# The start of a causal attention and feed-forward kernel: the first eight heads' q and k laid out by selection products, and the rest of the preparation put beside the first steps

## The chip, the core and the metric

The kernel runs on one core of a Trainium2 chip. The metric is device microseconds of one execution. A core has five engines, each with a queue of its own that it works through in order: PE (TensorE, the matrix products; its weight loads are listed as PEld), DVE (VectorE), ACT (ScalarE), POOL (GpSimd) and SP (SyncE, which here only issues transfers). PE writes to PSUM, eight banks of 512 float32 for each of 128 partitions; DVE and ACT read it there.

## The reference

x has 4096 tokens of 256 features. The attention has 16 heads of 16 features:

```python
x = x + layernorm(attention(layernorm(x)))      # causal, softmax(q k^T / 4) v, then w_proj, b_proj
h = silu((y @ w1.T) * w1_s) * ((y @ w2.T) * w2_s)     # y = layernorm(x)
h = gelu((h @ h1.T) * h1_s); h = gelu((h @ h2.T) * h2_s)
x = x + layernorm((h @ w3.T) * w3_s)
```

The feed-forward weights are ternary, w_attn and w_proj are float32, and the biases of the attention are random.

## The kernel before

**Blocks and items.** The tokens are cut into eight blocks j of 512 (NB = 8). The attention goes through 32 items (j, g): block j of the queries with the four heads of group g. An item has `count` = 4 (j + 1) steps, one for each tile of 128 keys. A step makes the scores of its four heads (two ScoreUnits of two heads, L641 to L693: products of k and q, then a product that subtracts the row's maximum, then ACT's exponential) and, two steps later, their products with v (Values, L695 to L727). The feed-forward (L910 on) follows after all items.

**Maxima.** The row maxima come from products of their own, by MaxUnit (L569 to L639): two products of 64 rows into two of the three banks of the pool ps_m, and DVE's maximum over each (L594, or L598 with the mask on the diagonal). Two units, one for each pair of heads, make a pair of the stream `maxima`. Pairs run ahead of the scores: `goal` (L874) lets the stream reach three pairs (LEAD) past the end of the next item, spread evenly over the item's steps. When an item's last pair is done, `to_rows` (L625) turns its maxima into a row with four products (pmt) and a copy (mrow, L638).

**The preparation of a block** is the generator `prep(j)` (L498 to L555): load x, take the layernorm statistics (DVE for blocks 0 and 1, ACT for the others), normalize (DVE for block 0, POOL for the rest), transpose on PE into xT (tile T), and then `features` (L421) for k and q, each in two halves c of eight heads, and the products pv with wv for v. `features` makes 128 features for 512 tokens, adds the bias on ACT (tile full), and splits the result into hi and lo, two parts that the fast product format holds exactly. Each part is written twice to a DRAM array `halves_of` by SP (L449), four transfers of 256 KB for each half c: a score product wants for each head the rows hi, lo, hi, lo of k against hi, hi, lo, lo of q, 64 rows a head. `load_rows` (L453) reads two heads, 128 rows, back into one tile: `queries` two tiles for an item, `keys` two tiles for an item and a key block, into a ring of 16 slots (tags k0_0 to k15_1). `queries` of item n + 2 is called at the head of item n, and `ask` (L484) loads keys up to item n + 2. All these loads and sends stand in SP's one queue.

**Order.** Past L786 the order of each engine's queue is the order of the program text (a schedule written out by hand). Before the change it is: the product of v's bias with wp, added to bp (L829 to L838); prep(0); queries and keys for items 0 and 1; prep(1), all of it; seven pairs of maxima (L847); then the items (L852). Within an item, `Background` (L23) holds generators (preparations, projections) with a size in pieces; `bg.pace` (L898) advances as many pieces after each step as are needed to be done in time. A generator can yield BESIDE between products, where `unit_beside` (L816) may put a unit of maxima (only for blocks 1 to 6). prep(j + 2) is added in block j's first item at its third step and has to be done at the head of block j's last item (L855). project(j) (L208), the output projection, is added when the block's last values are stored.

Records: a float32 product appears in the profile as two records, so 16 records named pk and pq are eight products, the k and q features of one block.

Of the kernel before, what the change touches and what calls it, by code (L numbers as in the profile page):

```python
# [10 lines left out]
F32 = mybir.dt.float32  # L11
# [56 lines left out]
def sandwich_kernel(  # L68
# [116 lines left out]
    def piece(tag, name, dtype=F32):  # L185
        return pieces.tile([P, QB], dtype, tag=tag, name=name)
# [151 lines left out]
    with ExitStack() as actx:  # L338
# [13 lines left out]
        def two_banks(name):  # L352
            return ps_s.tile([P, 2, QB], F32, tag="s", name=name)

        class Room:
# [5 lines left out]
            def features(self, j):  # L361
                return [wk1.tile([P, DC, QB], F32, tag=t, name=f"{t}o_{j}") for t in ("o", "T")]
# [4 lines left out]
        wqk = [piece(f"wqk{d}", f"wqk{d}") for d in range(DC)]  # L367
        for d in range(DC):
            nc.scalar.dma_start(out=wqk[d], in_=w_attn[d * P : (d + 1) * P, 0 : 2 * D])
        wv = aw.tile([P, DC, D], F32, tag="wv", name="wv")  # L370
        nc.scalar.dma_start(
            out=wv, in_=w_attn[:, 2 * D : 3 * D].rearrange("(c p) f -> p c f", p=P)
        )

        bv = aw.tile([P, DC], F32, tag="bv", name="bv")
        nc.scalar.dma_start(out=bv, in_=b_attn[2 * D : 3 * D].rearrange("(c p) -> p c", p=P))

        bqk = aw.tile([P, 2 * DC], F32, tag="bqk", name="bqk")
        nc.scalar.dma_start(out=bqk, in_=b_attn[0 : 2 * D].rearrange("(s p) -> p s", p=P))
        nc.vector.tensor_scalar(bqk[:, 0:DC], bqk[:, 0:DC], SCALE, None, ALU.mult)  # L380

        two = aw.tile([P, 2], F32, tag="two", name="two")
        nc.vector.tensor_reduce(
            two,
            ident.rearrange("p (i pr e) -> p pr i e", i=2, pr=2)[:, :, :, 0:2],
            AX.XY,
            ALU.add,
        )
        identr = aw.tile([P, P], F32R, tag="identr", name="identr")
        nc.vector.tensor_copy(identr, ident)  # L390
        ones = [aw.tile([P, P], F32R, tag=f"ones{pr}", name=f"ones{pr}") for pr in range(2)]
        for pr in range(2):
            nc.vector.tensor_copy(ones[pr], two[:, pr : pr + 1].to_broadcast([P, P]))

        nc.scalar.dma_start(out=wp, in_=w_proj.rearrange("(c p) f -> p c f", p=P))
        nc.scalar.dma_start(out=bp, in_=b_proj.partition_broadcast(P))

        mask = aw.tile([P, QB], F32, tag="mask", name="mask")
        nc.gpsimd.memset(mask, 0.0)
# [18 lines left out]
            for j in range(NB)  # L418
        }

        def features(j, s, c, engine):  # L421

            i = "qk".index(s)
            ps = two_banks(f"p{s}_{j}_{c}")[:, 0, :]
            for d in range(DC):
                nc.tensor.matmul(  # L426
                    ps,
                    lhsT=wqk[d][:, i * D + c * P : i * D + (c + 1) * P],
                    rhs=xTs[j][:, d, :],
                    start=(d == 0),  # L430
                    stop=(d == DC - 1),
                )
                yield Background.BESIDE
            full = piece(f"full{c % 2}", f"full{s}_{j}_{c}")
            nc.scalar.activation(
                full,
                ps,
                AF.Identity,
                bias=bqk[:, i * DC + c : i * DC + c + 1],
                scale=1.0 if i else SCALE,  # L440
            )
            hi = piece(f"hi{c % 2}", f"hi{s}_{j}_{c}")
            engine.tensor_copy(hi.bitcast(F32R), full)
            lo = piece(f"lo{c % 2}", f"lo{s}_{j}_{c}")
            engine.tensor_tensor(lo.bitcast(F32R), full, hi.bitcast(F32R), ALU.subtract)
            for half, part in enumerate((hi, lo)):
                for d in range(2):
                    at = (d, half) if i else (half, d)
                    nc.sync.dma_start(  # L449
                        out=halves_of[s, j][8 * c : 8 * (c + 1), at[0], at[1]], in_=part  # L450
                    )

        def load_rows(tag, name, key, j, h):  # L453

# [7 lines left out]
        def query(tag, name, dtype):  # L462
            return qp.tile([P, QB], dtype, tag=tag, name=name)
# [31 lines left out]

        xTs = {}

        def prep(j, engine=nc.gpsimd):  # L498

            xj = xb[j] if j in xb else load_block(j)  # L500
            for _ in range(3):
                yield True
            mv = stat.tile([P, NT, 2], F32, tag="mv", name=f"mv_{j}")
            ahead = j < 2
            for t in range(NT):
                if ahead:
                    layernorm_stats(xj[:, t, :], mv, t)
                else:
                    mean_of(xj[:, t, :], mv, t)
                    yield True  # L510
                    spread_of(xj[:, t, :], mv, t)
                yield True
            v_j = kv.tile([P, NT, H * VW + HD], F32, tag=f"v{j}", name=f"v{j}")
            vb.append(v_j)
            nc.gpsimd.memset(v_j[:, :, H * VW :], 0.0)
            v_heads = v_j[:, :, 0 : H * VW].rearrange("p t (h e) -> p t h e", e=VW)
            nc.gpsimd.memset(v_heads[:, :, :, HD:VW], 1.0)
            rstd = (layernorm_rstd if ahead else rstd_of)(mv)
            for t in range(NT):
                (normalize if ahead else shift_and_scale)(  # L520
                    xj[:, t, :], xj[:, t, :], mv, rstd, t, engine
                )
                yield True
            for _ in range(3):
                yield True
            xT = xTs[j] = wk1.tile([P, DC, QB], F32, tag="T", name=f"xT_{j}")
            ps = two_banks(f"pt_{j}")
            for c in range(DC):
                for t in range(NT):
                    nc.tensor.transpose(  # L530
                        ps[:, c, t * P : (t + 1) * P], xj[:, t, c * P : (c + 1) * P], ident
                    )
            nc.scalar.copy(xT, ps)  # L533
            yield True
            for s in "kq":
                for c in range(DC):
                    yield from features(j, s, c, engine)
                    yield True
            for half in range(0, NT, 2):
                ps = two_banks(f"pv_{j}_{half}")[:, 0, :].rearrange("p (t f) -> p t f", t=2)  # L540
                for t in range(2):
                    for c in range(DC):
                        nc.tensor.matmul(  # L543
                            ps[:, t, :],
                            lhsT=xT[:, c, (half + t) * P : (half + t + 1) * P],
                            rhs=wv[:, c, :],
                            start=(c == 0),
                            stop=(c == DC - 1),
                        )
                    yield Background.BESIDE  # L550
                nc.scalar.copy(
                    v_heads[:, half : half + 2, :, 0:HD],
                    ps.rearrange("p t (h d) -> p t h d", d=HD),
                )
                yield True  # L555
# [260 lines left out]
        def unit_beside():  # L816
# [4 lines left out]
            if begun_pair:  # L821
                issue(MaxUnit(*begun_pair.pop(0)))

        values = Values()
        W = {}
        alone = cycle((False, False, True))
        issued = now = 0

        ps = two_banks("pb")[:, 0, 0:D]  # L829
        for c in range(DC):  # L830
            nc.tensor.matmul(
                ps,
                lhsT=bv[:, c : c + 1].to_broadcast([P, P]),
                rhs=wp[:, c, :],
                start=(c == 0),
                stop=(c == DC - 1),
            )
        nc.vector.tensor_tensor(bp, bp, ps, ALU.add)  # L838
        for j in range(2):
            work = prep(j, (nc.vector, nc.gpsimd)[j])  # L840
            while bg.piece(work) is not False:
                pass
            if j == 0:
                for n in range(2):
                    queries(*items[n])
                    keys(*chunks[n])
        while issued < first[1] + LEAD:  # L847
            for args in next(stream):
                issue(MaxUnit(*args))
            issued += 1  # L850
        rows_of(now + 4)
        for n, (j, g) in enumerate(items):  # L852
            if n + 2 < len(items):
                queries(*items[n + 2])
            if g == G - 1 and j + 2 < NB:  # L855
                bg.finish(("prep", j + 2))

            if (j, g) == (NB - 2, 0):
# [15 lines left out]
            goal = min(first[min(n + 2, len(items))] + LEAD, first[-1])  # L874
            for kt in range(count[n]):
                ask(n, kt)
                if (g, kt) == (0, 2) and j + 2 < NB:
                    bg.add(("prep", j + 2), prep(j + 2), PREP)
                due = begun + (goal - begun) * (kt + 1) // count[n] - issued
                pairs = [next(stream) for _ in range(due)]  # L880
# [14 lines left out]
                now += 2  # L895
                values.add(j, g, kt, max(kt - NT * j, 0) * P, es, now - 1)
                rows_of(now)
                bg.pace(count[n] - kt + count[n] * max(G - 2 - g, 0))  # L898
                if j > 0 and kt % 4 == 2 and kt < NT * j:
                    next(halving, None)  # L900
            rows_of(now + 2)
# [232 lines left out]
```

## Time and profile before

| | us |
|---|---|
| three runs | 2493.22, 2483.43, 2488.50 |
| median | 2488.5 |
| the profiled execution: its time | 2495.86 |
| its span, first to last instruction | 2494.2 |
| PE busy (share of the span) | 2395.7 (96%) |
| DVE busy | 1786.7 (72%) |
| ACT busy | 1309.1 (52%) |
| POOL busy | 561.6 (23%) |
| mean granted clock of PE | 0.975 |

The profile is of one execution. A line of its timeline has the start in us, the length in us, the engine (SPq and ACTq are the transfers that these engines issue), the line of the kernel, the operation, out<-in, and how many were merged; in brackets stands how long the engine was idle before it and what ended that wait. In the windows, each engine's busy time in a stretch is followed by the number of its instructions; the clock is what PE was granted, 1.00 being full. A busy PE may run at half rate. The page's slices cut the span into 40 equal parts of 62.4 us, with the busy share and the clock in tenths.

### The profile page before, as it was taken

Reading aid. Unit: us, or ns where it says so; the run is one execution under the profiler, and the core shown is the slowest. Engines: PE = TensorE matmul, PEld = TensorE weight load, DVE = VectorE, ACT = ScalarE, POOL = GpSimd, SP = SyncE. Lnnn points to the kernel's source line nnn. Section 1 sums busy time; section 2 is a strip of 40 time slices with the busy share of each in tenths; the row PEclk is TensorE's granted clock in tenths of the full one; section 3 lists DMA queues with packets and bytes.
Section 4 is the critical chain, followed back from the end, with each engine's and each line's share of the span. In section 5 each row is a group of like instructions: output and inputs, shape, how many; then the busy total and the mean of one; then the engine's idle time right before and its main releaser. Section 6 shows DMA issues by size and latency. Waiting matters only on the chain.

```text
span 2494.2 us, 40139 instructions
## 1 busy us (share of the span) xinstructions
PE 2395.7 (96%) x15237; PEld 1434.2 (58%) x15237; DVE 1786.7 (72%) x3838; ACT 1309.1 (52%) x1710; POOL 561.6 (23%) x898
## 2 busy tenths in 40 slices
PE   4899999999999999999999999999999999999998
PEld 2545545545554555455555555544488787887887
DVE  1667988888897989799999888986145535554553
ACT  1336666665675667666667667766822222222221
POOL 2325333423343233322422222000001200000000
PEclk8779999999999999999999999999999999999999
DMA  4444434323333322424222231111111100000000
GB/s 145 150 141 141 151 115 152 120 82 130 107 126 117 116 72 96 151 94 133 84 74 72 88 109 60 51 56 56 47 54 35 34 1 18 17 17 1 17 9 10
DMA packets 134825, 202.73 MB, mean 81 GB/s; under 512 B 14912, under 2 KB 59584, under 8 KB 134624
## 3 DMA queue, kind: packets, MB, share of 16 engines
q1 hardware_dynamic: 132672, 198.75, 24.3%
q8 instruction: 122, 2.00, 0.3%
q10 hardware_dynamic: 1776, 1.18, 0.2%
q14 instruction: 79, 0.65, 0.1%
q0 software_dynamic: 176, 0.15, 0.1%
HBM read 137.91 MB, written 62.13 MB: 80 GB/s over the span
## 4 chain that ended last, share of the span: by engine, by line
PE 82%; DVE 11%; issue 2%; DMA 2%; ACT 1%; POOL 1%; SPq 0%; ACTq 0%; POOLq 0%; DVEq 0%
PE av L714 20%; PE s L664 18%; PE z L1007 18%; PE pm L581 16%; DVE mx L594 3%; DVE pm L598 2%; PE pyf L1076 2%; DVE fa L1048 2%; PE pk L426 1%; PE py L249 1%; PE pv L543 1%; PE pq L426 1%; PE pmt L630 1%; PE za L1007 1%; PE zb L1007 1%
## 5 line engine op out<-in xcount | busy, mean ns | idle before, releaser
L679 ACT ACTIVATE e<-s 128x1024 f32<-128x1024 f32 (+3 forms) x1175 | 1039.1, 936 | 471.1 <-PE s L664 462.3
L594 DVE TENSOR_REDUCE mx<-pm 128x1 f32<-128x512 f32 x1792 | 1111.5, 682 | 153.0 <-PE pm L581 135.4
L581 PE MATMUL pm<-k,q 64*128 64x512 f32 (+3 forms) x2304 | 626.9, 456 | 33.0 <-DVE mx L594 18.6
L581 PEld LDWEIGHTS pm<-k,q 64*128 64x128 f32 x2304 | 325.1, 188 | 533.3 <-DVE mx L594 368.9
L714 PE MATMUL av<-e,v 128*32 128x512 f32 (+3 forms) x4608 | 582.5, 577 | 0.2 <-POOL e L684 0.2
L664 PE MATMUL s<-q,k 64*128 64x512 f32 (+3 forms) x2304 | 472.7, 391 | 4.4 <-ACT xT L533 1.2
L664 PE MATMUL s<-mrow,ones 64*128 64x512 f32 (+3 forms) x2304 | 458.9, 381 | 0.0
L598 DVE CUSTOM_DVE_ANT_0 pm<-pm,mask 128x384 f32<-128x384 f32 (+3 forms) x512 | 240.2, 517 | 78.6 <-PE pm L581 75.7
L1063 ACT ACTIVATE fb<-z,sh 128x512 f32<-128x512 f32 x128 | 88.1, 688 | 388.4 <-PE z L1007 367.2
L664 PEld LDWEIGHTS s<-q,k 64*128 64x128 f32 x2304 | 236.5, 189 | 71.7 <-issue 18.8
L664 PEld LDWEIGHTS s<-mrow,ones 64*128 64x128 f32 x2304 | 241.3, 189 | 38.3 <-DVE mrow L638 0.7
L684 POOL TENSOR_SCALAR_AFFINE_SELECT e<-e 128x256 f32<-128x256 f32 x256 | 102.3, 407 | 620.1 <-ACT e L679 618.0
L1007 PE MATMUL z<-hb_0h,h 128*128 128x512 f32 x512 | 200.8, 392 | 0.0
L1007 PE MATMUL z<-hb_0l,h 128*128 128x512 f32 x512 | 200.0, 391 | 0.0
L714 PEld LDWEIGHTS av<-e,v 128*32 128x32 f32 x4608 | 91.7, 108 | 143.6 <-issue 130.5
L173 POOL TENSOR_TENSOR rstd<-ve,neghalf 128x4 f32<-128x4 f32 (+1 forms) x22 | 20.7, 943 | 662.9 <-DVE ve L171 637.4
L977 DVE CAST hb_1h<-fb 128x512 fp32r<-128x512 f32 x64 | 27.8, 435 | 144.5 <-ACT fb L1063 144.5
L977 DVE CAST hb_0h<-fb 128x512 fp32r<-128x512 f32 x64 | 27.3, 427 | 138.7 <-ACT fb L1063 138.7
L1007 PEld LDWEIGHTS z<-hb_0h,h 128*128 128x128 f32 x512 | 96.8, 189 | 20.0
L1046 ACT ACTIVATE sl<-za,s 128x512 f32<-128x512 f32 x64 | 44.0, 689 | 122.2 <-PE za L1007 64.2
L1007 PEld LDWEIGHTS z<-hb_0l,h 128*128 128x128 f32 x512 | 96.7, 189 | 19.9
L1048 DVE SCALAR_TENSOR_TENSOR fa<-zb,s,sl 128x512 f32<-128x512 f32 x64 | 47.6, 745 | 72.2 <-ACT sl L1046 72.2
(247 smaller groups left out, 2437.8 us busy)
## 6 DMA issues: line engine op xcount, KB each, us to landing
k<-k SPq DMA_DIRECT2D x288, 256.0 KB
q<-q SPq DMA_DIRECT2D x64, 256.0 KB
x<-in_x_dram SPq DMA_DIRECT2D x16, 512.0 KB
k<-hik SPq DMA_DIRECT2D x32, 256.0 KB
k<-lok SPq DMA_DIRECT2D x32, 256.0 KB
q<-hiq SPq DMA_DIRECT2D x32, 256.0 KB
q<-loq SPq DMA_DIRECT2D x32, 256.0 KB
avd<-av_sb SPq DMA_DIRECT2D x32, 256.0 KB
```

Source lines behind the costliest of these rows:

```text
L426: nc.tensor.matmul(ps, lhsT=wqk[d][:, i * D + c * P : i * D + (c + 1) * P], rhs=xTs[j][:, d, :], start=(d == 0), stop=(d == DC - 1),)
L581: nc.tensor.matmul(ps[:, 0:n], lhsT=qT[j, g][pr][r, t * P : (t + 1) * P], rhs=kT[G * j + g, c, pr][r, 0:n], start=True, stop=True,)
L594: nc.vector.tensor_reduce(self.mx[:, h, c : c + 1], ps[:, 0:n], AX.X, ALU.max)
L598: nc.vector.tensor_tensor_reduce(out=ps[:, 0:n], in0=ps[:, 0:n], in1=mask[:, QB - n : QB], scale=1.0, scalar=-3.0e38, op0=ALU.add, op1=ALU ...
L664: nc.tensor.matmul(self.ps[i][:, self.q0 :], lhsT=(self.k, ones[pr])[m][r, :], rhs=(qT[j, g][pr], mT[j, g])[m][r, self.q0 :], start=(m == ...
L679: nc.scalar.activation(e[:, at : at + n, q0:], ps[:, :, q0:], AF.Exp)
L684: nc.gpsimd.affine_select(out=at, in_=at, compare_op=ALU.is_ge, fill=0.0, base=0, pattern=[[0, 2], [1, P]], channel_multiplier=-1,)
L714: nc.tensor.matmul(self.av[h * HW : (h + 1) * HW, q0:], lhsT=vb[kt // NT][:, kt % NT, o : o + HW], rhs=es[h // 2][:, h % 2, q0:], start=(k ...
L977: nc.vector.tensor_copy(hi, full)
L1007: nc.tensor.matmul(ps, lhsT=w[c], rhs=single(part[:, c, :]), start=(c == 0 and i == 0), stop=(c == kc - 1 and i == parts - 1),)
L1048: nc.vector.scalar_tensor_tensor(h, zb, s2[:, oc : oc + 1], sl, ALU.mult, ALU.mult)
L1063: nc.scalar.activation(h, z, AF.Gelu, scale=sc[:, oc : oc + 1])
```

## The change

1. The product that adds v's bias to bp goes from the head of the program into a function `bias_of_v`, called at item 1. Its inputs wp, bv and bp are no longer loaded on ACT's queue at the start but on SP's, after q of block 0. The q and k biases (bqk) are loaded before wv. The small constants (`two`, `identr`, `ones`, and the scaled bqk, now on ACT) are made after block 0's transposes.
2. `prep` is cut into `turned` (load to transposes), the features, and `values_of`. Only block 0 takes its statistics on DVE now.
3. Block 0's k and q of heads 0 to 7 (c = 0) don't go through DRAM to items 0 and 1. `at_home` multiplies hi and lo by `sel`, matrices of zeros and ones, in products of 32 rows (two heads of 16 features) and adds hi's and lo's product in PSUM, so that each of four banks gets the 128 rows of a pair of heads in their final order. ACT and DVE copy the banks to the tiles of items 0 and 1. k of these heads is still sent to DRAM, for the later blocks, q isn't. sel, hi and lo borrow slots 13 to 15 of the ring of keys.
4. `rest` makes c = 1 of k and q (POOL splits them) and v of block 0, with two units of maxima at each BESIDE, for the first five pairs of the stream (before: seven pairs, with nothing beside).
5. prep(1) becomes background work of items 0 and 1. prep(2) is added at item 2 instead of item 0 and has to be done at the head of item 6 instead of item 3. The pace is counted by `ends`.

The diff, cut to its core:

```diff
-        nc.scalar.dma_start(out=wp, in_=w_proj.rearrange("(c p) f -> p c f", p=P))
-        nc.scalar.dma_start(out=bp, in_=b_proj.partition_broadcast(P))
...
-        def features(j, s, c, engine):
+        def features(j, s, c, engine, tags=None, then=send):
...
+            then(j, s, c, (hi, lo))
...
-            ahead = j < 2
+            ahead = j < 1
...
+        def ends(n):
+
+            if n < G:
+                return first[2] if n < 2 else first[G + 2]
+            return first[max(n, n // G * G + G - 2) + 1]
...
+        sel = piece("k13_0", "sel", F32R)
+        nc.gpsimd.memset(sel.bitcast(F32), 0.0)
+
+        def select():
+            row = piece("k13_1", "row")[:, 0:HW]
+            nc.vector.tensor_reduce(row, ident.rearrange("p (m c) -> p c m", m=4), AX.X, ALU.add)
+            rows2 = row.rearrange("p (i d) -> p i d", i=2)
+            for i in range(2):
+                for half in range(2):
+                    at = (2 * i + half) * P
+                    to = sel[:, at : at + P].rearrange("p (i a b d) -> p i a b d", i=2, a=2, b=2)
+                    for e in range(2):
+                        a, b = (e, half) if i else (half, e)
+                        nc.vector.tensor_copy(to[:, :, a, b, :], rows2)
+
+        def at_home(j, s, c, parts):
+
+            i = "qk".index(s)
+            banks = [two_banks(f"home{s}_{n}") for n in range(2)]
+            for half, part in enumerate(parts):
+                at = (2 * i + half) * P
+                for m in range(4):
+                    r = slice(32 * m, 32 * (m + 1))
+                    nc.tensor.matmul(
+                        banks[m // 2][:, m % 2, :],
+                        lhsT=sel[r, at : at + P],
+                        rhs=part.bitcast(F32R)[r, :],
+                        start=(half == 0),
+                        stop=(half == 1),
+                    )
+            for n in range(2):
+                for pr in range(2):
+                    if i:
+                        t = kT[n, 0, pr] = piece(f"k{n}_{pr}", f"k{n}_0_{pr}", F32R)
+                    else:
+                        t = query(f"q{pr}", f"q{pr}_0_{n}", F32R)
+                        qT.setdefault((0, n), []).append(t)
+                    (nc.vector.tensor_copy if pr else nc.scalar.copy)(t, banks[n][:, pr, :])
+            if i:
+                asked[0] = 2
...
+        for _ in turned(0, nc.vector):
+            pass
+        consts()
...
+        for s, slot in (("k", 15), ("q", 14)):
+            for _ in features(0, s, 0, nc.vector, (f"k{slot}_0", f"k{slot}_1"), keep):
                 pass
-            if j == 0:
-                for n in range(2):
-                    queries(*items[n])
-                    keys(*chunks[n])
-        while issued < first[1] + LEAD:
-            for args in next(stream):
-                issue(MaxUnit(*args))
-            issued += 1
+        nc.sync.dma_start(out=wp, in_=w_proj.rearrange("(c p) f -> p c f", p=P))
+        nc.sync.dma_start(out=bv, in_=b_attn[2 * D : 3 * D].rearrange("(c p) -> p c", p=P))
+        nc.sync.dma_start(out=bp, in_=b_proj.partition_broadcast(P))
+
+        def rest():
+
+            for s, tags in (("k", ("hi1", "lo1")), ("q", ("hi0", "lo0"))):
+                yield from features(0, s, 1, nc.gpsimd, tags)
+            send(0, "k", 0, kept["k"])
+            yield from values_of(0)
+
+        units = deque(args for _ in range(first[1] + 1) for args in next(stream))
+        issued = first[1] + 1
+        for beside in rest():
+            for _ in range(2 * (beside == Background.BESIDE and bool(units))):
+                issue(MaxUnit(*units.popleft()))
+        while units:
+            issue(MaxUnit(*units.popleft()))
         rows_of(now + 4)
+        bg.add(("prep", 1), prep(1), PREP)
         for n, (j, g) in enumerate(items):
+            if n == 1:
+                bias_of_v()
+            if n in (2, G + 2):
+                bg.finish(("prep", n // G + 1))
             if n + 2 < len(items):
                 queries(*items[n + 2])
-            if g == G - 1 and j + 2 < NB:
+            if g == G - 1 and 0 < j < NB - 2:
                 bg.finish(("prep", j + 2))
...
-                if (g, kt) == (0, 2) and j + 2 < NB:
+                if (g, kt) == ((0, 2) if j else (2, 0)) and j + 2 < NB:
                     bg.add(("prep", j + 2), prep(j + 2), PREP)
...
-                bg.pace(count[n] - kt + count[n] * max(G - 2 - g, 0))
+                bg.pace(ends(n) - first[n] - kt)
```

More of the change, by code (lines that the diff above doesn't have):

```diff
@@ L369, in sandwich_kernel @@
             nc.scalar.dma_start(out=wqk[d], in_=w_attn[d * P : (d + 1) * P, 0 : 2 * D])
+        bqk = aw.tile([P, 2 * DC], F32, tag="bqk", name="bqk")
+        nc.scalar.dma_start(out=bqk, in_=b_attn[0 : 2 * D].rearrange("(s p) -> p s", p=P))
         wv = aw.tile([P, DC, D], F32, tag="wv", name="wv")
@@ L375, in sandwich_kernel @@
         bv = aw.tile([P, DC], F32, tag="bv", name="bv")
[L376 to L380, printed above, removed]
         two = aw.tile([P, 2], F32, tag="two", name="two")
[L383 to L388, printed above, removed]
         identr = aw.tile([P, P], F32R, tag="identr", name="identr")
-        nc.vector.tensor_copy(identr, ident)
         ones = [aw.tile([P, P], F32R, tag=f"ones{pr}", name=f"ones{pr}") for pr in range(2)]
-        for pr in range(2):
-            nc.vector.tensor_copy(ones[pr], two[:, pr : pr + 1].to_broadcast([P, P]))
-        nc.scalar.dma_start(out=wp, in_=w_proj.rearrange("(c p) f -> p c f", p=P))
-        nc.scalar.dma_start(out=bp, in_=b_proj.partition_broadcast(P))
         mask = aw.tile([P, QB], F32, tag="mask", name="mask")
@@ L419, in sandwich_kernel, with send @@
         }
-        def features(j, s, c, engine):
+        def send(j, s, c, parts):
+            for half, part in enumerate(parts):
+                for d in range(2):
+                    at = (d, half) if s == "k" else (half, d)
+                    nc.sync.dma_start(
+                        out=halves_of[s, j][8 * c : 8 * (c + 1), at[0], at[1]], in_=part
+                    )
+        def features(j, s, c, engine, tags=None, then=send):
             i = "qk".index(s)
@@ L441, in features @@
             )
-            hi = piece(f"hi{c % 2}", f"hi{s}_{j}_{c}")
+            tags = tags or (f"hi{c % 2}", f"lo{c % 2}")
+            hi = piece(tags[0], f"hi{s}_{j}_{c}")
             engine.tensor_copy(hi.bitcast(F32R), full)
-            lo = piece(f"lo{c % 2}", f"lo{s}_{j}_{c}")
+            lo = piece(tags[1], f"lo{s}_{j}_{c}")
             engine.tensor_tensor(lo.bitcast(F32R), full, hi.bitcast(F32R), ALU.subtract)
[L446 to L451, printed above, removed]
+            then(j, s, c, (hi, lo))
         def load_rows(tag, name, key, j, h):
@@ L496, in sandwich_kernel, with prep, turned @@
         xTs = {}
-        def prep(j, engine=nc.gpsimd):
+        def prep(j):
+            yield from turned(j)
+            for s in "kq":
+                for c in range(DC):
+                    yield from features(j, s, c, nc.gpsimd)
+                    yield True
+            yield from values_of(j)
+        def turned(j, engine=nc.gpsimd):
             xj = xb[j] if j in xb else load_block(j)
@@ L534, in prep, with values_of @@
             yield True
[L535 to L538, printed above, removed]
+        def values_of(j):
+            xT = xTs[j]
+            v_heads = vb[j][:, :, 0 : H * VW].rearrange("p t (h e) -> p t h e", e=VW)
             for half in range(0, NT, 2):
@@ L827, in sandwich_kernel @@
         issued = now = 0
[L829 to L836, printed above, removed]
-            )
[L838 to L841, printed above, removed]
-                pass
-            if j == 0:
-                for n in range(2):
-                    queries(*items[n])
-                    keys(*chunks[n])
@@ L847, in sandwich_kernel, with bias_of_v @@
-        while issued < first[1] + LEAD:
-            for args in next(stream):
-                issue(MaxUnit(*args))
-            issued += 1
+        def bias_of_v():
+            ps = two_banks("pb")[:, 0, 0:D]
+            for c in range(DC):
+                nc.tensor.matmul(
+                    ps,
+                    lhsT=bv[:, c : c + 1].to_broadcast([P, P]),
+                    rhs=wp[:, c, :],
+                    start=(c == 0),
+                    stop=(c == DC - 1),
+                )
+            nc.vector.tensor_tensor(bp, bp, ps, ALU.add)
@@ new lines, in at_home @@
+        def at_home(j, s, c, parts):
+            i = "qk".index(s)
+            banks = [two_banks(f"home{s}_{n}") for n in range(2)]
+            for half, part in enumerate(parts):
+                at = (2 * i + half) * P
+                for m in range(4):
+                    r = slice(32 * m, 32 * (m + 1))
+                    nc.tensor.matmul(
+                        banks[m // 2][:, m % 2, :],
[3 more added lines that the diff above has]
+                        stop=(half == 1),
+                    )
+            for n in range(2):
[8 more added lines that the diff above has]
+                asked[0] = 2
@@ new lines, in consts @@
+        def consts():
+            nc.scalar.mul(bqk[:, 0:DC], bqk[:, 0:DC], SCALE)
+            select()
+            nc.vector.tensor_reduce(
+                two,
+                ident.rearrange("p (i pr e) -> p pr i e", i=2, pr=2)[:, :, :, 0:2],
+                AX.XY,
+                ALU.add,
+            )
+            nc.vector.tensor_copy(identr, ident)
+            for pr in range(2):
+                nc.vector.tensor_copy(ones[pr], two[:, pr : pr + 1].to_broadcast([P, P]))
+        for _ in turned(0, nc.vector):
+            pass
@@ new lines, in sandwich_kernel, with keep @@
+        consts()
+        kept = {}
+        def keep(j, s, c, parts):
+            kept[s] = parts
+            at_home(j, s, c, parts)
+        for s, slot in (("k", 15), ("q", 14)):
+            for _ in features(0, s, 0, nc.vector, (f"k{slot}_0", f"k{slot}_1"), keep):
+                pass
+        nc.sync.dma_start(out=wp, in_=w_proj.rearrange("(c p) f -> p c f", p=P))
+        nc.sync.dma_start(out=bv, in_=b_attn[2 * D : 3 * D].rearrange("(c p) -> p c", p=P))
+        nc.sync.dma_start(out=bp, in_=b_proj.partition_broadcast(P))
```

## The prediction

> **What bounds the kernel now.** I read the page's slices first: where is TensorE not the bound?
>
> ```profile
> PE   4899999999999999999999999999999999999998
> PEclk8779999999999999999999999999999999999999
> ```
>
> From the fourth slice on PE is busy nine tenths at a clock of nine tenths or more. Only the first three slices (62.4 us each) show slack, as idle time (slice one) and as a low granted clock (two and three). A change to the start can win there and nowhere else, and work that it pushes past about 190 us costs its full price. Then the timeline of the start:
>
> ```profile
> 14.52 0.42 DVE L138 BATCH_NORM_STATS2 bn<-x 128x6 f32<-128x256 f32 x1
> 21.98 5.62 PE L426 MATMUL pk<-xT,wqk 128*128 128x512 f32 x8 [1.10 <-ACT xT L533]
> ...
> 44.96 4.84 POOL L177 TENSOR_SCALAR x<-x,mv,rstd 128x256 f32<-128x256 f32 x4
> ...
> 46.24 0.48 PE L530 MATMUL pt<-ident,x 128*128 128x128 f32 x1 [11.75 <-POOL x L177]
> ...
> 64.93 0.43 PE L581 MATMUL pm<-k,q 64*128 64x128 f32 x3
> ...
> 65.29 0.30 DVE L598 CUSTOM_DVE_ANT_0 pm<-pm,mask 128x128 f32<-128x128 f32 x1 [21.54 <-PE pm L581]
> ```
>
> DVE starts the statistics only at 14.52, behind the addition to bp (L838), which waits for wp. The first maximum product (L581) stands at 64.93, behind all of block 1's preparation in PE's order; DVE is idle 21.5 us for it. Last, windows cut at the first score product of each item (before item 0, items 0, 1, 2, 3, 4, then 5 to 7; columns: stretch, length, then busy time with count of PE, PEld, DVE, ACT, POOL, then clock, DMA share, GB/s):
>
> ```profile
> 64.90:79.90 15.00, 13.10 (x35) 7.64 (x36) 14.15 (x67) 0.59 (x1) 3.15 (x3) 0.68 0.57 214
> 79.90:95.60 15.70, 13.03 (x78) 7.62 (x76) 9.42 (x39) 6.15 (x11) 3.24 (x8) 0.55 0.35 116
> 95.60:109.70 14.10, 12.33 (x86) 7.31 (x85) 9.92 (x43) 9.14 (x23) 6.80 (x16) 0.69 0.34 120
> 109.70:133.20 23.50, 21.96 (x126) 12.18 (x124) 10.45 (x30) 10.13 (x16) 8.99 (x14) 0.97 0.47 165
> 133.20:156.30 23.10, 21.34 (x102) 10.65 (x102) 18.72 (x56) 6.27 (x10) 4.71 (x11) 0.62 0.59 208
> 156.30:190.60 34.30, 30.62 (x189) 15.79 (x187) 24.27 (x71) 17.59 (x32) 8.21 (x12) 0.86 0.22 71
> 190.60:270.00 79.40, 77.06 (x540) 40.19 (x540) 63.95 (x171) 49.71 (x78) 34.78 (x62) 1.00 0.45 157
> ```
>
> Item 2 carries block 2's preparation beside its steps: 23.5 us at clock 0.97, against 14.1 at 0.69 for item 1 with the same four pairs. So **a preparation beside early steps costs 9.4 us**. Alone (block 1: 46.24 to 64.93) it costs 18.7.
>
> **The change, part by part** (profiled execution: 2495.9 us, span 2494.2; the median of the three runs is 7.4 lower).
>
> *Start.* bp's sum leaves DVE's head, and wp, bv and bp leave ACT's queue. Block 0's x is the first DMA of SP. One-microsecond windows moved 16, 158, 341, 396, 379, 350 and 172 GB/s from 1 to 8 us, together 1.81 MB, the size of x0, x1, wqk and wv (1.84 MB); I take 7 us for x0 (5.5 to 8.5). From the first statistics to pk's start is 7.4 us in the rows, so pk starts at 14.4. The new constants (13 small DVE instructions of 0.15 to 0.25 us, one small one on ACT) lie beside transposes, copy and products, 5 us in which DVE is idle; uncovered they cost 2.
>
> *k and q at home.* Products until ACT starts 3.83 (21.98 to 25.81, at half rate: records 0.85 us apart, later 0.43), bias 0.71, hi 0.47, lo 0.69. The selection products are not in the trace: eight of 32 rows and 512 columns for each of k and q, the last four after lo. Two 64-row products of that width together take 0.43 us at half clock (79.90 to 80.33), and four 32-column ones do run together (L714), so I take 0.43 plus 0.2 to drain; one after another they would be 1.7. Copies out 0.69 (as L638, 0.69; ACT's as L551, 0.59). That is 6.33 for k until the copies, 0.69 until a buffer is free for q, 6.33 and 0.69 again, and 1.7 for the next feature product ahead of the first unit: 15.7. The first maximum product comes at 14.4 + 15.7 = **30.1** (27 if the clock rises early, 34 with serial products and late x0).
>
> *Ten units beside the rest of block 0.* Ten units alone took 64.93 to 75.15, 10.2 us, DVE-bound. Beside them PE has eight records of k and q of c = 1 and sixteen of values: 7 us at full rate, 14 at half. Bounds 10 and 24; I take 16, nearer the lower since each product lies beside DVE's work. First score at **46.5** instead of 79.9: **-33.4**.
>
> *Item 0* issues six pairs instead of four. Item 3's two-pair steps take 5.8 each, item 1's one-pair steps 3.5: 2 x 5.8 + 2 x 3.5 = 18.6 against 15.7, **+2.9** (0 to 6). Its loads of heads 8 to 11 stand behind twelve sends and wp, bv, bp on SP; at 1.2 us a send they are issued near 52, land near 56, and are asked for near 56: no wait, where before there was one of 2.7.
>
> *Item 1* takes block 1's preparation (steps 5 to 7 by the pace: 26 pieces over eight steps) and bp's four records (2.05 us): 23.5 + 2 - 14.1 = **+11.4** (3 to 21). Block 1's statistics go from DVE to ACT, as block 2's did in items 0 and 1 before; that is within the windows used.
>
> *Item 2* loses block 2's preparation: 14.1 instead of 23.5, -9.4. But its second step asks for block 1's q and k, which now have a short way to go:
>
> ```profile
> 117.68 1.22 SPq L449 DMA_DIRECT2D k<-hik  x2
> ...
> 134.44 2.41 SPq L449 DMA_DIRECT2D q<-loq  x2
> 136.95 2.27 SPq L456 DMA_DIRECT2D q<-q  x2
> ```
>
> Sixteen sends fill SP until 22.7 us after block 2's first product (114.26); 2 less with denser pieces. Loads of q and k behind them need some 8 us to land (k issued at 78.57 released PE at 84.91, 6.3, after 2 of q's issue). That is 28.7 after the first product. PE comes there after 18.9 less one step plus one step, 18.9. A **stall of 10 us** (3 to 15): everything on PE is behind it. Sum **+0.6**. Item 3 is unchanged in work: 0.
>
> *Items 4 to 7* now take the product part of block 2's preparation (the pace gives items 2 and 3 only its waits and statistics, ten pieces), besides block 0's projection and block 3's preparation as before. PE prices from block 3's, at full clock:
>
> ```profile
> 236.83 3.70 PE L426 MATMUL pq<-xT,wqk 128*128 128x512 f32 x8
> ...
> 242.72 3.50 PE L543 MATMUL pv<-wv,xT 128*128 128x256 f32 x15
> ```
>
> With k like q and 1.06 for transposes that is 12. Item 4 has slack: 34.3 us against 30.62 x 0.86 = 26.3 of PE at full clock, 8 us, part of it DVE waiting 2.6 for the sums of the projection; I take 5.3 as filled. **+6.7** (4 to 18.7). After 270 us PE is the bound and nothing differs.
>
> Sum: -33.4 + 2.9 + 11.4 + 0.6 + 6.7 = **-11.8**, so 2484.1 for such an execution and **2476.7** as a median.
>
> [...] The rows: items 0 and 1 ran at 0.55 and 0.69 though PE waited at most 2.7 us at a time. [...]
>
> **Rivals.** *Hidden work*: with more on PE the clock stays up from 30 us on, as in item 2 (0.97), and the stall is its lower bound. The unit phase is then 12 instead of 16, item 1 costs 6 less (PE warm in steps 4 and 5 too), the stall 7 less: 17 more won, 2460. For it: every stretch with preparation in it is warm. Against: ten units alone ran at 0.68.
>
> *Handed back*: the head start is real, but SP's queue gives out at its own pace. With a stall of 15 (+5), loads for item 0's third step 4 late, and 3 less filled in item 4: 12 less, 2489. For it: PE has already waited once for such a load. A change that does not do what it says, the first unit not before 42, gives the same.
>
> *Slower than before*: the two preparations moved beside steps cost what one costs alone, 18.7 each, because their products wait on ACT's and POOL's turn (copy of xT, hi and lo) with everything behind them. +9.3 and +12.0: 2498. It decides from 11.8 us over the 16.1 that I took for both. Against: item 2 shows 9.4.
>
> **Numbers.** Forecast 0.5 (2468 to 2485 as its own spread), hidden 0.2, handed back 0.16, slower 0.14. The measurement tells about 0.5% (12.4 us) from no change, so faster by that means under 2476.1: nearly half of the forecast and all of the hidden case, 0.44. Slower means over 2500.9, just past the last rival's price: over half of that case, and a little of the one handed back, 0.09. The rest is 0.47. The range leaves out the ends of the outer cases: 2459 to 2495.
>
> **What would show it.** First maximum product near 30 and first score near 46.5; 32-row products in fours within about half a microsecond; PE idle some 10 us before item 2's second step, released by a DMA of q or k; item 4 warmer than 0.86. I am wrong if no such wait shows, if the clock before item 3 is 0.9, or if items 4 to 7 grow by over 12 us.

## The result, and the profile after

The changed kernel takes 2524.1 us (median of five, 2519.6 to 2530.0) against 2489.0 for the kernel before (five runs): 1.0136 of it, 95% interval 1.0123 to 1.0150. Faster by 12 was forecast; it is 35 slower. The profiled execution took 2519.6 us, the lowest of its five (span 2517.8), while that of the kernel before, 2495.9 us, lies above all of its five; so the two traces differ by 23.8 us only.

The page's slices of the changed kernel:

```profile
PE   6796999999999999999999999999999999999998
...
PEclk8787999999999999999999999999999999999999
```

The first slice is fuller than before (6 instead of 4), but the second and the fourth are worse (7 instead of 8, 6 instead of 9), and the clock is low into the fourth. So the start was gained and more was lost between 60 and 250 us. The timeline of the start:

```profile
5.31 0.43 DVE L138 BATCH_NORM_STATS2 bn<-x 128x6 f32<-128x256 f32 x1 [5.31 <-DMA x<-in_x_dram]
...
13.26 3.78 PE L420 MATMUL pk<-xT,wqk 128*128 128x512 f32 x4 [1.10 <-ACT xT L532]
18.38 0.80 PE L872 MATMUL homek<-hik,sel 32*128 32x512 f32 x4 [1.33 <-DVE hik L438]
...
30.92 0.69 PE L581 MATMUL pm<-k,q 64*128 64x128 f32 x3
...
35.92 2.07 PE L420 MATMUL pq<-xT,wqk 128*128 128x512 f32 x2
...
53.56 0.50 PE L664 MATMUL s<-q,k 64*128 64x512 f32 x2
```

The first maximum product comes at 30.9 (64.9 before), the first score product at 53.6 (79.9 before). A feature product between the units (two records) takes 2.07 us, and one of four records at 13.26 took 3.78: 0.85 us a record, half of the rate that later records show (0.43).

Where the lead goes is seen from the copy of each item's weighed values and sums (L723), shortly after its last scores:

| item | before, us | after, us | difference |
|---|---|---|---|
| 0 | 98.3 | 75.7 | -22.6 |
| 1 | 112.7 | 101.7 | -11.0 |
| 3 | 159.5 | 148.5 | -11.0 |
| 4 | 193.4 | 198.5 | +5.1 |
| 5 | 215.2 | 243.1 | +27.9 |
| 6 | 251.7 | 282.4 | +30.7 |
| 7 | 273.0 | 304.0 | +31.0 |
| 31 | 1797.4 | 1820.8 | +23.4 |

Items 4 to 7 lose 42 us, items 4 and 5 alone 39. After item 9 (+31.9) the difference falls by more than 0.3 us only in items 10, 27, 28 and 30, where the trace of the kernel before had the lower clock (0.94 to 0.98, against 0.99 to 1.00 in the other trace) and PE waited for the same things as long, to 0.3 us. So the loss of the change is made in the first eight items, and 31 of the 35 us can be read there. Windows cut 2.2 us ahead of these copies, one for each of items 4 to 7, first of the kernel before, then of the changed one (columns as in the prediction):

```profile
157.30:191.20 33.90, 30.22 (x191) 15.73 (x188) 23.87 (x69) 18.16 (x34) 8.21 (x12) 0.87 0.23 72
191.20:213.00 21.80, 21.11 (x168) 11.06 (x166) 19.57 (x57) 17.34 (x35) 12.86 (x26) 1.00 0.43 142
213.00:249.50 36.50, 35.36 (x216) 18.08 (x214) 24.37 (x65) 18.34 (x24) 16.99 (x27) 1.00 0.42 145
249.50:270.80 21.30, 20.79 (x167) 11.12 (x165) 19.77 (x52) 13.46 (x17) 5.64 (x13) 1.00 0.55 191
```

```profile
146.30:196.30 50.00, 40.72 (x222) 19.86 (x220) 29.57 (x82) 18.84 (x26) 14.03 (x22) 0.88 0.32 110
196.30:240.90 44.60, 29.18 (x196) 15.12 (x194) 23.08 (x68) 18.38 (x35) 17.39 (x28) 0.81 0.31 94
240.90:280.20 39.30, 33.54 (x196) 17.77 (x196) 17.35 (x41) 22.80 (x41) 14.84 (x24) 0.92 0.34 120
280.20:301.80 21.60, 20.17 (x162) 10.76 (x161) 19.16 (x51) 13.27 (x17) 7.96 (x17) 1.00 0.61 216
```

Of PE's time in these four items, the idle part (length less busy) grows from 6.0 to 31.9 us; the busy time times the clock, an estimate of the work at full rate (two records of a feature product took 2.07 us at a clock of 0.50, at 35.92, and eight 3.70 at 1.00, at 236.83 in the kernel before), from 103.6 to 110.5; what a low clock costs by it (busy time less that product) from 3.9 to 13.1. So of 42 us **26 are idle time, 9 a low clock, and only 7 work that was moved here**. PE's waits in these items, in the changed kernel (who, released by whom: total, times, longest):

```profile
PE pm L581 <- DMA k<-k: 13.8, 2, 8.1
PE pm L581 <- DVE mx L594: 7.6, 3, 6.4
PE av L714 <- POOL e L684: 5.0, 3, 3.2
```

And the timeline of the two longest, of SP's queue, DVE and PE:

```profile
182.26 2.39 SPq L411 DMA_DIRECT2D q<-loq  x2
...
185.87 1.36 SPq L222 DMA_DIRECT2D sums<-avd  x1
...
192.06 0.55 DVE L225 RECIPROCAL sums<-sums 128x64 f32<-128x64 f32 x1 [5.84 <-DMA sums<-avd]
193.22 0.79 PE L581 MATMUL pm<-k,q 64*128 64x512 f32 x1 [6.36 <-DVE mx L594]
...
196.99 2.29 SPq L446 DMA_DIRECT2D k<-k  x4
...
206.58 0.80 PE L581 MATMUL pm<-k,q 64*128 64x512 f32 x2 [8.12 <-DMA k<-k]
```

Block 2's last sends are followed on SP by the load of block 0's sums. DVE stands on that load with its reciprocal, and PE stands on DVE's maxima. Once PE gets on it stands on loads of k that were called a step earlier; these no longer stood behind a send, the last of which passed SP at 184.65.

### The profile page after: what moved, and what is told of

It is laid out like the page before. It is cut to its first block, busy times and chain, and to the rows that moved or that the text cites. A ratio compares the mean times of both kernels' runs of the same rounds, so it can differ in the third digit from the quotient of the medians.

```text
span 2517.8 us, 40162 instructions
## 1 busy us (share of the span) xinstructions
PE 2396.7 (95%) x15253; PEld 1430.5 (57%) x15253; DVE 1789.0 (71%) x3837; ACT 1315.4 (52%) x1731; POOL 563.6 (22%) x904
## 3 DMA queue, kind: packets, MB, share of 16 engines
q1 hardware_dynamic: 131664, 196.00, 23.8%
## 4 chain that ended last, share of the span: by engine, by line
PE 79%; DVE 11%; DMA 3%; issue 3%; ACT 2%; POOL 1%; SPq 1%; POOLq 0%; ACTq 0%; DVEq 0%
PE av L714 19%; PE z L1095 18%; PE s L664 18%; PE pm L581 16%; DVE mx L594 3%; DVE pm L598 2%; PE pyf L1164 2%; DVE fa L1136 2%; PE py L249 1%; PE pk L420 1%; PE pv L543 1%; DMA k<-k 1%; ACT e L679 1%; PE pq L420 1%; PE pmt L630 1%
```

## The experiments

Ratios are to the kernel before, in the same set, with their intervals. Theory L is that block 2's late preparation costs the time, rival S that the start does.

**Block 2 early** (from the changed kernel):

```diff
-                return first[2] if n < 2 else first[G + 2]
+                return first[2] if n < 2 else first[G]
...
-            if n in (2, G + 2):
+            if n in (2, G):
```

> Block 2's preparation back into items 2 and 3 (done at the head of item 4), the rest as in the changed kernel. Theory L (the loss is block 2's preparation in items 4 to 6, with the sends and the pairs of maxima that it brings): items 4 to 7, 156 us from the first score of item 4 to that of item 8 in the changed kernel against 114 before, fall back to about 115, and items 2 and 3 grow by 5 to 12 us; in all 30 to 37 us less than the changed kernel, 0.985 to 0.988 of it, so at or a little under the kernel before (0 to 6 us less). Rival S (the start itself, selection products and a preparation beside items 0 and 1, disturbs what follows): less than 10 us gained.

Measured 1.0039 (1.0027 to 1.0052): 24 us less than the changed kernel. Items 5 to 7 are back to 21.8, 36.5 and 21.2 us. But item 4 takes 42.4 and item 3 grew by 10.2; the waits in item 4:

```profile
DVE sums L225 <- DMA sums<-avd: 12.0, 1, 12.0
PE pm L581 <- DVE mx L598: 11.9, 1, 11.9
```

Theory L carries two thirds of the loss. What is left is 10 us over the kernel before: the lead is spent by the end of item 3 (its copy comes at 158.8, before at 159.5), and item 4 loses 8.5 more by the wait for the sums, which here too are loaded behind block 2's sends, six loads of q and k and the store of block 0's last values (SP issued that store at 165.24 and the load of the sums at 171.00).

**The kernel before, block 2 late**:

```diff
...
+            if n == G + 2:
+                bg.finish(("prep", 2))
...
-            if g == G - 1 and j + 2 < NB:
+            if g == G - 1 and 0 < j < NB - 2:
...
-                if (g, kt) == (0, 2) and j + 2 < NB:
+                if (g, kt) == ((0, 2) if j else (2, 0)) and j + 2 < NB:
...
-                bg.pace(count[n] - kt + count[n] * max(G - 2 - g, 0))
+                bg.pace(ends(n) - first[n] - kt)
```

> The kernel before, with its start untouched, and only block 2's preparation moved as the change moves it (added at item 2, paced to the head of item 6). Theory L: item 2 gets shorter by some 9 us, items 4 to 7 longer by some 40, so 25 to 35 us slower than the kernel before. Rival S: within 8 us of the kernel before, as block 2's products cost about what they cost anywhere (12 us in items 4 and 5 against 9.4 in item 2).

Measured 1.0127 (1.0104 to 1.0150), 32 us slower with the start untouched. (`ends` is that of the changed kernel.) Item 2 falls from 23.0 to 11.2 us, items 4 to 7 grow from 113.5 to 160.4, with the same waits, their totals to 0.4 us:

```profile
PE pm L581 <- DMA k<-k: 14.1, 2, 8.2
PE pm L581 <- DVE mx L594: 8.0, 3, 6.6
PE av L714 <- POOL e L684: 5.0, 3, 3.2
```

Undoing the move takes 24 us away, doing it alone adds 32: the move is the main cause, shown from both sides.

**No units beside block 1's background** (changed kernel):

```diff
-            if not begun_pair and 1 <= j < NB - 1 and g < G - 1 and len(ahead) < NT:
+            if not begun_pair and 2 <= j < NB - 1 and g < G - 1 and len(ahead) < NT:
```

> The changed kernel with no unit of maxima put beside background products while block 1 is at work (begins with block 2). Theory A (the four pairs taken ahead in item 4 let the stream ask for the tiles of item n + 2 one step after their loads are called): PE's waits of 8.1 and 5.7 us for loads of k at the heads of items 5 and 6 go, 10 to 20 us gained. Rival Q (those loads are late only because sixteen sends and the projection's transfers stand before them on SP): the waits move to the steps that then ask for k, and less than 5 us is gained.

Measured 1.0142 (1.0121 to 1.0164): nothing gained. The two waits for k did go, but others came, and item 7, which then had the pairs not taken before, took 30.5 us instead of 21.6. PE's waits in items 4 to 7 now:

```profile
PE pm L581 <- DVE mx L594: 8.1, 3, 7.0
PE av L714 <- POOL e L684: 7.1, 4, 2.8
PE s L664 <- ACT e L679: 4.4, 4, 3.8
PE py L249 <- POOL oo L239: 3.8, 1, 3.8
```

My theory A, that pairs taken ahead cost 10 to 20 us, falls: they only choose which wait is met. Rival Q, with waits for k at a later step, is not what came either.

**Sums later** (changed kernel):

```diff
-        for _ in range(5 if 1 < j < NB - 1 else 3):
+        for _ in range(5 if 1 < j < NB - 1 else 12 if j == 0 else 3):
```

> The changed kernel with block 0's projection waiting twelve pieces instead of three between the load of its sums and the reciprocal on DVE. If the 6.4 us in which PE waited for DVE's maxima in item 4 are the reciprocal standing on DVE for that load behind block 2's sends, they go, and 4 to 9 us are gained. If the time is lost by DMA traffic in any case, the next wait for k takes them: under 2 us.

Measured 1.0084 (1.0057 to 1.0111), 13 us less than the changed kernel, more than expected. PE's wait of 6.4 us for DVE is gone; what is left of it in items 4 to 7:

```profile
PE pm L581 <- DVE mx L594: 1.4, 2, 1.0
```

Item 4 takes 42.4 instead of 50.0 and item 5 36.9 instead of 44.6; item 6 gives 7.7 back.

**Both remedies** (block 2 early and sums later):

> Both remedies of the first set: block 2's preparation in items 2 and 3, and block 0's projection waiting twelve pieces before its reciprocal. With block 2 early, DVE stood 12.0 us on the reciprocal, whose load of sums stood on SP behind block 2's sends and six loads, and PE 11.9 us on DVE. Theory: that wait goes and nothing else comes; item 4 falls from 42 us to 34, as in the kernel before; 8 to 12 us less than with block 2 early alone, so 0.999 to 1.001 of the kernel before. Rival: PE next waits for a transfer in its place (the projection's own loads), under 4 us gained.

Measured 1.0046 (1.0030 to 1.0062), no gain on block 2 early alone. Item 4 did fall, from 42.4 to 32.4 us, but item 5, in which the projection now stands, rose from 21.8 to 32.9 and item 6 by 3.0. Over items 4 to 7 PE's idle time fell from 15.9 to 12.2 us against block 2 early alone, while what a low clock costs rose from 4.6 to 10.8. So the wait did go, and a lower clock in items 4 and 6 (0.78 and 0.91, with block 2 early alone 0.84 and 1.00) and waits in item 5 took what it gave.

**No lead at item 2** (both remedies, and `LEAD * (n != 2)` in the goal, L874 of the kernel before):

> As the run with both remedies, and in item 2 the stream of maxima stops at item 4 (no lead of three pairs), so that block 1's q and k are first asked for in item 3. Theory (the 10.4 us of PE in item 2 are the way of block 1's q and k through DRAM, and the step that asks is too near): the wait goes, items 2 and 3 together lose 6 to 11 us; 0.995 to 0.998 of the kernel before. Rival: item 3, with eleven pairs instead of eight, is bound by DVE (some 27 us of maxima beside block 2's products) and gives it back, under 3 us gained.

Measured 1.0099 (1.0083 to 1.0115), worse by 13 us. The wait for k in item 2 is gone, and PE waits 11.4 us for ACT instead: ACT, with block 2's statistics in its queue, stands on block 2's x, which SP loads behind the same sends (in the changed kernel x goes at 109.75, the last send passed at 103.49). With both remedies ACT stood on it as well, for 12.9 us, beside PE's wait for k; so one wait had hidden another.

```profile
ACT junk L144 <- DMA x<-in_x_dram: 13.8, 1, 13.8
```

Item 2 takes 28.6 us and item 3 44.2, both longer than with both remedies (23.2 and 33.7).

**The start alone** (changed kernel, block 1's preparation in one piece ahead of the items, block 2's as in the kernel before):

```diff
-        bg.add(("prep", 1), prep(1), PREP)
+        work = prep(1)
+        while bg.piece(work) is not False:
+            pass
...
```

> The change's start alone: q and k of the first eight heads by selection products, ten units of maxima beside the rest of block 0; then block 1's preparation in one piece ahead of the first step, and block 2's from item 0's third step to item 3, both as before. If the start by itself is worth what the first score shows (53.6 us instead of 79.9, less 18.7 to 22 for block 1 in one piece), 4 to 8 us under the kernel before, 0.997 to 0.9985. If the selection products and SP's fuller queue cost more than they bring, over 1.001.

Measured 1.0045 (1.0028 to 1.0061): the start by itself is 11 us slower than the kernel before, though its first score comes 4 us sooner, at 75.9. PE's two long waits in item 0:

```profile
84.05 2.28 PE L714 MATMUL av<-e,v 128*32 128x512 f32 x8 [4.68 <-POOL e L684]
...
95.67 0.47 PE L581 MATMUL pm<-k,q 64*128 64x128 f32 x2 [6.97 <-DMA k<-k]
```

The first: POOL's selects for the scores stand in its queue behind block 1's lo, which waits 2.3 us and more for earlier sends to leave its tile. The second: loads of heads 8 to 11 stand behind sixteen sends. The rest is work of PE's own: from the first score to some 2 us ahead of item 0's copy there are 32.1 us instead of 16.1, and PE was idle for 12.9 of them (2.7 before) and busy for 19.2 (13.4 before), with two pairs of maxima more and bp's sum (2.07 us) in it. So the lead was spent before item 1: item 0's copy comes at 110.0, before at 98.3.

**Block 1 sooner** (both remedies, and block 1 paced over six steps):

```diff
-                return first[2] if n < 2 else first[G]
+                return first[1] + 2 if n < 2 else first[G]
...
-                bg.pace(ends(n) - first[n] - kt)
+                bg.pace(max(ends(n) - first[n] - kt, 1))
```

> As the run with both remedies, and block 1's preparation paced over six steps instead of eight, so that its products and sends come some two steps, 7 us, sooner. If the wait in item 2 is the age of those sends, it falls from 10.4 us to 2 to 6 and 4 to 8 us are gained on the run with both remedies. If transfers are bound by their rate (256 KB in 1.2 us) with the loads of items 2 and 3 among them, less than 2.

Measured 1.0030 (1.0016 to 1.0044), 4 us less than with both remedies, which the two intervals don't part. The wait in item 2 fell from 10.2 to 7.0, less than expected.

**Sends on POOL's queue** (block 1 sooner, `nc.gpsimd.dma_start` in `send`):

> As the run with both remedies and block 1 sooner, with the sends of hi and lo issued on POOL's queue, so that loads of q, k, x and sums on SP no longer stand behind them. Theory H (the lost time is loads standing behind sends in SP's one queue): PE's waits for k, for the affine selects and for x (7 us and several of 2 to 4 in the first 320 us) go and 10 to 20 us are gained on the run with block 1 sooner; about 0.995 to 0.999 of the kernel before. Rival W (the sends themselves are bound by their rate, 256 KB in 1.2 us, and loads share it): under 4 us gained, or lost where POOL's issue of some 1 us a send delays its selects.

Measured 1.0111 (1.0088 to 1.0135), worse by 20 us. The longest wait for k fell to 5.1, but POOL now spends 0.6 us on each issue, and PE waits for its selects, 7.15 us at once:

```profile
PE av L714 <- POOL e L684: 14.7, 6, 7.2
```

POOL's issues delaying its selects is what rival W's second half foresaw. Whether a queue that does nothing else would help stays open.

**The head alone** (the kernel before, with bp's sum, its loads, bqk and the constants where the change puts them):

> The kernel before with only the head of the change: wp, bv and bp loaded on SP, bp's sum at item 1, bqk ahead of wv, and the constants after block 0's transposes. q and k go through DRAM, block 1's and block 2's preparation stand where they stood. The statistics start at 5.3 instead of 14.5 in the changed kernel. Theory H: all of the start moves 9 us forward together, sends and loads with it, so 6 to 10 us less than the kernel before, 0.996 to 0.9975. Rival C (the gain is handed back later, as in the other runs): within 3 us.

Measured 0.9956 (0.9939 to 0.9974), 11 us faster. Block 1's first product comes at 43.2 instead of 52.3:

```profile
43.20 5.21 PE L420 MATMUL pk<-xT,wqk 128*128 128x512 f32 x8 [1.10 <-ACT xT L532]
```

Items 0 to 3 move with it (their last copy comes at 146.1 instead of 159.5). Item 4 gives 4 us back, 38.0 instead of 33.9, with PE waiting up to 3.1 for the projection's inputs from POOL.

**Head and tags** (the head alone, and block 0's q in tiles of its own):

```diff
-                for _ in features(0, s, c, nc.vector):
+                tags = (f"k{14 + c}_0", f"k{14 + c}_1") if s == "q" else None
+                for _ in features(0, s, c, nc.vector, tags):
```

> As the run with the head alone, and hi and lo of block 0's q in tiles of their own (slots 14 and 15 of the ring of keys), so that DVE no longer waits 2 to 3 us at a time for the sends of k before it may write q's (in the kernel before 9.7 us, which block 1's statistics stand behind). If the sends are what sets block 1's start, nothing: 0 to 2 us. If DVE's order is, block 1's products and the first maxima come 6 to 8 us sooner, 4 to 8 us gained on the head alone.

Measured 0.9947 (0.9929 to 0.9965), the lowest ratio of all these runs, 13 us under the kernel before. Block 1's first product comes 7.4 us sooner than with the head alone. Only part of it stays: its interval overlaps that of the head alone, and the wait for k in item 0 grew from 2.9 to 5.6.

**Selection products in the old order** (head, `at_home` for the first eight heads, the rest of block 0 on DVE, then as in the kernel before):

> The head of the change and its selection products, with everything else in the order of the kernel before: the rest of block 0 on DVE, then block 1's preparation in one piece, seven pairs of maxima, block 2's preparation from item 0's third step. Against the run with head and tags this differs by the selection products alone: 16 rows of k and q make two stops of PE (about 8 us each before block 1 can start), and SP has 4 sends and 8 loads fewer. If the products only lengthen the path to block 1's start (21 us of PE's first 29 in the changed kernel were for half of k and q), 2 to 6 us slower than head and tags, 0.996 to 0.998 of the kernel before. If the fewer transfers decide (the wait of 5.6 us for k in item 0), 2 to 6 us faster, 0.992 to 0.994.

Measured 0.9984 (0.9972 to 0.9995): about 9 us slower than head and tags. The first product of block 1 in head and tags, then here:

```profile
35.85 5.46 PE L420 MATMUL pk<-xT,wqk 128*128 128x512 f32 x8 [1.10 <-ACT xT L532]
```

```profile
48.48 5.50 PE L420 MATMUL pk<-xT,wqk 128*128 128x512 f32 x8 [1.10 <-ACT xT L532]
```

PE stops for ACT and DVE (1.3 us idle ahead of 18.36, 1.4 of 21.20, 1.3 of 26.26, 1.4 of 28.89) and makes only half of k and q by 25 us, so all that follows is 12.6 us later. The fewer transfers win some of it back (the wait for k is 2.7 instead of 5.6).

## Why the prediction was wrong, point by point

*Start up to the first unit: right.* x0 was there at 5.3 (7 was taken), pk started at 13.3 (14.4), four selection products took 0.80 us (0.43 and 0.2) behind feature products of 0.85 us a record, the first maximum product came at 30.9 (30.1). DVE's copies waited for ACT's (DVE idle 1.5 us ahead of k's and 1.2 of q's), which I had side by side. Two misses cancel here: pk came 1.1 us sooner, and the stretch from it to the first maximum product was 17.7 us instead of 15.7. The sum itself has a slip: 30.1 and 16 make 46.1, not 46.5.

*Ten units beside block 0: mis-sized.* 22.6 us from 30.9 to the first score instead of 16. PE and DVE took turns (DVE idle 1.8 to 2.0 us ahead of each two of the first eight units) at a clock of 0.52: the stretch came near the upper bound of 24. The head start was 26.3 us, not 33.4, which is 7 us of the miss.

*Items 0 to 3: right.* Item 0 took 19.4 (18.6), item 1 24.1 (25.5), item 2 25.3 (24.1) with a wait of 10.7 for k (10), item 3 23.0 (23.1). The windows of items 0 to 2, and the wait:

```profile
53.50:72.90 19.40, 16.79 (x92) 9.28 (x92) 14.42 (x60) 9.30 (x25) 6.33 (x15) 0.74 0.42 139
72.90:97.00 24.10, 22.15 (x128) 12.54 (x126) 9.63 (x40) 10.34 (x16) 9.11 (x14) 0.93 0.27 91
97.00:122.30 25.30, 12.03 (x87) 6.51 (x83) 10.02 (x30) 7.58 (x16) 5.10 (x11) 0.66 0.55 196
```

```profile
112.38 0.80 PE L581 MATMUL pm<-k,q 64*128 64x512 f32 x2 [10.74 <-DMA k<-k]
```

Block 1's preparation beside steps cost 10.0 (24.1 less item 1's 14.1), bp's sum among it; the last rival, 18.7 for each preparation, had the sign right and the mechanism wrong.

*Items 4 to 7: the step that failed.* I wrote +6.7, "5.3 as filled" of item 4's slack. It is +42. The work moved was not what was missed (12 by the rows, 7 by the windows as work at full rate): 26 of the 42 are idle time and 9 a low clock, and the term held neither. I counted the preparation's products and not its sixteen sends, though I had worked out for item 2 that such sends fill SP for 20 us. In items 2 and 3 of the kernel before they ended before block 0's sums were asked for (136.9 and 162.3); in item 4 they stand ahead of the sums, and so of the projection's loads, which wait for the reciprocal. With more pieces between that load and the reciprocal 13 us came back. I also left out the four pairs of maxima that are taken beside block 2's products: they bring the stream to the k of items 7 and 8 a step after its loads are called, which is the 13.8 us of waits for k. Without these pairs other waits came in their place, and PE's idle time in items 4 to 7 was still 29.1 us. And I read item 4's slack as room, when part of it was DVE's 2.6 us wait for those sums, the first sign of what got longer. The bound of 18.7 that I gave, a preparation alone, holds no wait of others behind it.

*Handed back:* the nearest rival. It named SP's queue and a stall, in item 2, for 12 us; the stall came where it was put, at 10.7 us instead of its 15, and the larger toll came in items 4 and 5, for which it had 3.

*The clock: as the row had it.* Item 2 without its preparation was priced by item 1's row, 14.1 us at 0.69; less its wait of 10.7 it took 14.6, in a window at 0.66. In item 3 of the changed kernel PE waited at most 0.4 us at a time and ran at 0.62; what holds the clock down there no run shows:

```profile
122.30:145.30 23.00, 21.23 (x102) 11.01 (x103) 19.10 (x57) 7.55 (x17) 3.48 (x10) 0.62 0.40 130
```

*What stays open:* how the 26 us of idle time divide among transfers, DVE and POOL, since most waits taken away brought another; and whether the loads are late by their place in SP's queue or by the rate of the sends, since the one run with another queue put the sends on an engine that had work of its own.

## What to carry to other kernels

Work that is moved takes its transfers with it: list whose loads stand behind its sends in the same queue at the new place, and which engine stands on each of those loads, before pricing its arithmetic. An early first result is worth only what the next inputs allow; here the head of the change, which moved the start by 9 us, won 11 us by itself, and the parts built on it in the change cost more than that. Where one wait after another takes the place of the last, something may lie behind them all (here SP's queue or the sends' rate, which no run parts), and taking away single waits shows little of it.

## What the runs showed of the hardware

Four products of 32 rows and 512 columns into four banks ran together: 0.80 us for the four at 18.38 of the changed kernel, behind feature products of 0.85 us a record, and 0.51 at 26.28; two of 64 rows took 0.63 at a clock of 0.50 (80.33 in the kernel before). Sends of 256 KB passed SP at 0.6 us each at first (162.31 of the changed kernel: 1.21 us for two) and at 1.2 us each once some were under way (182.26: 2.39 for two), which is about 218 GB/s. In the window from 133.2 to 156.3 us of the kernel before, 208 GB/s went with a busy share of the DMA engines of 0.59. A send issued on POOL's queue kept POOL for 0.6 us, in the run with the second queue.
